# Loads ahead of stores and packing in pieces in a macaron FFN kernel with 4-bit weights

## The chip, the core and the metric

The kernel runs on one core of a Trainium2 chip. A core has a matrix engine (TensorE; PE in the profile, PEld for its weight loads), VectorE (DVE), ScalarE (ACT), GpSimd (POOL) and SyncE (SP), which runs nothing but DMA issues here. Each engine executes its own stream of instructions in order; a semaphore holds an instruction until what it needs is there. The metric is the device time of one execution in microseconds (us), lower is better. The kernel before took 2141.37 us, the median of 2140.46, 2141.37 and 2141.96.

## The reference

The input is `u`, 2 x 1024 tokens of 1024 channels, in f32. Three residual steps follow:

```python
x = u
x = x + 0.5 * ffn(layernorm(x))
x = x + s4(layernorm(x))
x = x + 0.5 * ffn(layernorm(x))

def ffn(x):                      # weights 4-bit, groups of 128 rows
    W = scale[group] * (nibble - (zero[group] + 1))
    return (silu(x @ Wg) * (x @ Wu)) @ Wd     # 1024 -> 2752 -> 1024
```

`s4` is a causal convolution along the 1024 positions with one kernel computed from a state-space model, plus `D[0] * x`. Both FFN calls use the same weights. A word of `qweight` (int32) holds eight nibbles, of eight consecutive rows of one column; `qzeros` packs eight columns a word.

## The kernel before, in words

The 2048 tokens are four blocks of 512. `JOBS` (L1345) lists eight jobs, one for each block and FFN. A job has a gate/up half (`gate_up`, L663) and a down half (`down`, L741). In gate/up, the 43 units of columns are cut into eight waves (`WAVES`, L38): five of six units of 128 columns, two of four, one of five. For each wave the eight groups of 128 input channels are walked (`STEPS`, L39, 64 steps); a step multiplies 512 tokens with the units of the wave for one group, twice (activations are split into a high part `xTh` and a low part `xTl`): 12 matmuls in the first five waves. After each group the partial sums in PSUM are rescaled in place by a ratio of scales (`scaled`, L657 to L661), by ACT for even units and by DVE for most odd ones. The rescaling must end before the next step adds to the same sum. The down half has 44 steps.

The nibbles are unpacked once, in the first job; this text calls it packing. For a wave: `fetch` loads the raw words (L454), `fetch_zeros` the zero points (L461) from a table that `zero_points` (L307) wrote to DRAM; `split` runs six DVE operations (`signed_bytes`, L501); `dequantize` (L541) copies one nibble of all words to bytes on POOL (`q`, L544) and SP stores these to DRAM (`wq`, L545), eight times a wave. A later step loads its 128 rows of bytes (`load_bytes`, L621, four steps ahead), and `make_weights` (three steps ahead) casts them to f32 weights `w_up`, on POOL (L637), or on ACT (L635) for three of eight steps in the first job. All jobs reload the bytes. The loads, stores, words, zero points and scales all stand in SP's one queue of issues. Pools: four `q` buffers, six for bytes, five for weights.

Hooks order this. `at(up, s, f)` runs `f` where step `s` is written; a framework's scheduler orders what the hooks emit by engine, except that `in_order_of_writing(f, engines)` keeps the written order on the engines named. `first_weights` (L579) places packing: a wave's `fetch` at step 8w-15, all six pieces of `split` at 8w-13, and the eight `dequantize` from 8w-12 on, one a step (w = 2 is a step or more off). The scales of later units are loaded (`scale_rows`, L326) in the opening and five steps before steps 16 and 32, and turned and inverted (`scales`, L336 on PE, then DVE) two steps before steps 4, 16 and 32.

`start` (L1519) is the opening, up to step 0, in written order on ACT, DVE, SP and PE. `first_split` splits wave 0's first group of rows in two halves of 16 bits; its `dequantize` copies the eight nibbles, odd ones on POOL (L493) and even ones on ACT (L495); SP stores each twice, 16 rows into the first tile of bytes (L496) and 128 rows to `wq` (L497). `first_moments` takes the layernorm sums of the four token tiles, 1 and 3 on ACT (L1467, L1468), 0 and 2 on DVE (L1473, L1474), then `deviations` the reciprocal roots on DVE. `first_rows` normalizes (ACT for odd tiles, L1488; DVE for even, L1490); `first_turn` transposes a chunk of 128 channels of all four tiles on PE (L1503), ACT makes the high part (L1504), DVE the low part (L1505). Turns 0 and 1 are in the opening; turns 2 to 7, and the rows of the second half of the channels, are hooks of steps 0 to 5 (`rows_by_chunk`, L1507).

Of the kernel before, what the change touches and what calls it, by code (L numbers as in the profile page):

```python
# [24 lines left out]
P = 128  # L25
# [30 lines left out]
def macaron_s4_kernel(  # L56
# [250 lines left out]
    def zero_points(which, z):  # L307

        p, n = z.shape
        zi, tab = (t2(f"{a}_{which}").bitcast(I32)[:p, : 8 * n] for a in ("zi", "ztab"))  # L310
        unpacked_zeros(tab, z, zi)
        dst, seg, queue = (zd_dram, SEGD, nc.sync) if which else (z_dram, SEG, nc.scalar)
        queue.dma_start(dst.rearrange("g (s n) -> (g s) n", s=seg), tab)

    def inverse(inv, s, name):

# [5 lines left out]
    def scale_rows(k0, k1, queue=nc.sync):  # L322
        n = k1 - k0
        row = t4(f"srow_{k0}") if n > 4 else t2(f"srow_{k0}")
        for m, src in enumerate((gate_s, up_s)):
            queue.dma_start(row[m * GK : (m + 1) * GK, : n * P], src[:, k0 * P : k1 * P])  # L326
        return row

    def scales(k0, k1, row):


        n = k1 - k0
        ps = bank(f"ps_s{k0}")
        u0, u1 = 2 * k0, 2 * k1
        for k in range(n):
            nc.tensor.transpose(  # L336
                ps[:, bass.ts(k, 2 * GK)], row[: 2 * GK, bass.ts(k, P)], ident[: 2 * GK, : 2 * GK]
            )
        if k1 == WIDE:
            row = t2("srow_half")  # L340
            for m, src in enumerate((gate_s, up_s)):
                nc.sync.dma_start(row[:GK, m * HALF : (m + 1) * HALF], src[:, WIDE * P :])
            nc.tensor.transpose(ps[:, bass.ts(2 * n, GK)], row[:GK, :P], ident[:GK, :GK])
            u1 = UNITS
        s = s_gu[:, u0:u1]
        flat = lambda a: a.rearrange("p u g -> p (u g)")
        nc.vector.tensor_copy(flat(s), ps[:, : (u1 - u0) * GK])
        inv = t2(f"inv_{k0}")[:, : (u1 - u0) * GK]
        inverse(inv, flat(s), k0)
        own = rat[:, u0:u1]  # L350
        inv = inv.rearrange("p (u g) -> p u g", g=GK)
        nc.vector.tensor_tensor(own[:, :, : GK - 1], s[:, :, : GK - 1], inv[:, :, 1:], ALU.mult)
        nc.vector.tensor_scalar(
            own[:, :, GK - 1 :], s[:, :, GK - 1 :], 1.0 / (EIGHT * LIFT), None, ALU.mult
        )
# [119 lines left out]
    def first_split(zq):  # L475


        n = width_of(0)
        z, zi, even = (t4(f"{a}_w0").bitcast(I32)[:, :n] for a in ("z", "zi", "even"))
        raw = packed.pop(0)[0]  # L480
        unpacked_zeros(z, zq, zi)
        nc.vector.tensor_scalar(even, raw, 3, NIBBLES, ALU.logical_shift_left, ALU.bitwise_and)
        nc.vector.tensor_scalar(raw, raw, 1, NIBBLES, ALU.logical_shift_right, ALU.bitwise_and)
        for part in (even, raw):
            both = part.bitcast(U16)
            nc.vector.tensor_tensor(both, both, z.bitcast(U16), ALU.add)
        nc.vector.tensor_scalar(both, both, 0x8080, None, ALU.bitwise_xor)

        def dequantize(j):
            q = qpool.tile([P, n], I8, tag="q", name=f"q_0_{j}")  # L490
            view = lambda a, dt: a.bitcast(dt).rearrange("p (n k) -> p k n", k=4)[:, j // 2, :]
            if j % 2:
                nc.gpsimd.tensor_copy(q, view(raw, I8))  # L493
            else:
                nc.scalar.activation(q, view(even, U8), AF.Identity, bias=minus_128)  # L495
            nc.sync.dma_start(first_tile[j:P:8], q[: P // 8])  # L496
            nc.sync.dma_start(w_q[0].rearrange("(r j) n -> j r n", j=8)[j], q)  # L497

        return dequantize

    def signed_bytes(key, raw, even, z):  # L501

        nc.vector.tensor_scalar(even, raw, 3, NIBBLES, ALU.logical_shift_left, ALU.bitwise_and)
        yield
        nc.vector.tensor_scalar(raw, raw, 1, NIBBLES, ALU.logical_shift_right, ALU.bitwise_and)
        yield
        for part in (even, raw):
            both = part.bitcast(U16)  # L510
            nc.vector.tensor_tensor(both, both, z.bitcast(U16), ALU.add)  # L511
            yield
            nc.vector.tensor_scalar(both, both, 0x8080, None, ALU.bitwise_xor)
            yield
        view = lambda a: a.bitcast(I8).rearrange("p (n k) -> p k n", k=4)
        packed[key] = view(even), view(raw)

    def split(w):
        raw, z = packed[w]
# [59 lines left out]
    def first_weights(up, dn, at):  # L579


        for w in range(1, len(WAVES)):
            s0 = 8 * w - 12 if w != 2 else 7
            if w > 1:
                both = lambda w=w: (fetch(w), fetch_zeros(w))
                at(up, s0 - 3, lambda both=both: in_order_of_writing(both, ET.SP))
                in_pieces(at, [(up, s0 - 1)], lambda w=w: split(w))
            else:
                both = lambda: [None for _ in split(1)]
                at(up, 0, lambda both=both: in_order_of_writing(both, *STARTING))  # L590
            for j in range(8):
                s = s0 + j if w > 2 else j // 2 + s0 * (w - 1)
                at(up, s, lambda w=w, j=j: dequantize(w, j))
        s0 = len(STEPS) - 12
        when = lambda n: (up, s0 + n) if n < 12 else (dn, (5 * (n - 12)) // 6)
        for n in range(6 * 8):
            k, j = divmod(n, 8)
            a, rt = divmod(k, 3)
            if j == 0:
                at(*when(max(0, n - 7)), lambda a=a, rt=rt: fetch_down(a, rt))  # L600
                steps = [when(max(0, n - d)) for d in (4, 3, 3, 2, 1, 0)]
                in_pieces(at, steps, lambda a=a, rt=rt: split_down(a, rt))
            at(*when(n), lambda a=a, rt=rt, j=j: dequantize_down(a, rt, j))
# [743 lines left out]
    def fast():  # L1347
        for j, (b, k) in enumerate(JOBS):
# [49 lines left out]
                    at(up, 4, store)  # L1398
            if j == 0:
                rows = {3: srow_next}  # L1400
                for s, k0, k1 in ((4, 3, 9), (16, 9, 15), (32, 15, WIDE)):
                    if k0 > 3:
                        load = lambda k0=k0, k1=k1: rows.update({k0: scale_rows(k0, k1)})
                        at(up, s - 5, load)
                    at(up, s - 2, lambda k0=k0, k1=k1: scales(k0, k1, rows.pop(k0)))
                at(up, 40, scales_down)
                zeros = lambda: zero_points(1, zeros_down)
                at(up, 12, lambda: in_order_of_writing(zeros, ET.DVE, ET.SP))
                for c in range(2, NC):
                    more = lambda c=c: rows_by_chunk(c)  # L1410
                    at(up, c - 2, lambda more=more: in_order_of_writing(more, *STARTING))
                first_weights(up, dn, at)
# [43 lines left out]
    STARTING = ET.Activation, ET.DVE, ET.SP  # L1456
    first = {}

    def first_moments():

        stats = small.tile([P, NT, 2, 6], F32, tag="stats", name="stats_0_1")
        mv = small.tile([P, NT, 2], F32, tag="mv", name="mv_0_1")
# [8 lines left out]
        for t in (0, 2):  # L1471
            for i in range(2):
                nc.vector.bn_stats(stats[:, t, i, :], x[0][t][:, bass.ts(i, 512)])  # L1473
            nc.vector.bn_aggr(mv[:, t, :], stats[:, t, :, :].rearrange("p a s -> p (a s)"))  # L1474
        nc.vector.tensor_scalar(mv[:, 1:4:2, 1], squares, 1.0 / HID, None, ALU.mult)
        guess(0, 1, mv)
        return mv, scratch

    def first_rows(t, lo, hi):

        half = lo // 512
        if lo % 512 == 0:
            first[t, half] = t2(f"xn_0_1_{t}_{half}")
        n = first[t, half][:, lo - 512 * half : hi - 512 * half]
        m, r, _ = ln[0, t]
        src = first["x"][t][:, lo:hi]
        if t % 2:
            nc.scalar.activation(n, src, AF.Identity, bias=first["bias"][:, t : t + 1], scale=r)  # L1488
        else:
            nc.vector.tensor_scalar(n, src, m, r, ALU.subtract, ALU.mult)  # L1490

    def first_turn(c):
# [8 lines left out]
        for t in range(NT):  # L1501
            src = first[t, c // 4][:, bass.ts(c % 4, P)]
            nc.tensor.transpose(ps[:, bass.ts(t, P)], src, ident)  # L1503
        nc.scalar.copy(hi, ps)  # L1504
        nc.vector.tensor_tensor(lo, ps, hi.bitcast(F32), ALU.subtract)  # L1505

    def rows_by_chunk(c):  # L1507
        if c < 4:
            for t in (2 * c - 4, 2 * c - 3):
                first_rows(t, 512, HID)  # L1510
        first_turn(c)

    def keep_warm(n, src=None):
# [5 lines left out]
    def start():  # L1519
# [8 lines left out]
        srow = scale_rows(0, 3)  # L1528
        zeros = zero_words(0)
        zeros_down = zero_words(1)  # L1530
        dequantize_first = first_split(zq)
        mv, scratch = first_moments()
        for j in (1, 3, 5, 7, 0, 2, 4, 6):
            dequantize_first(j)
        fetch(1)
        rows_next = scale_rows(3, 9)
# [10 lines left out]
            first_rows(t, P, 512)  # L1547
        scales(0, 3, srow)
        first_turn(1)
        zero_points(0, zeros)  # L1550
        fetch_zeros(1)
        return rows_next, zeros_down

    srow_next, zeros_down = in_order_of_writing(start, *STARTING, ET.PE)
# [88 lines left out]
```

## Time and profile before

| | us |
|---|---|
| median of the runs (three) | 2141.37 |
| the profiled execution | 2140.35 |
| its span | 2138.6 |
| PE busy | 2089.9 (98%) |
| DVE busy | 1700.3 (80%) |
| ACT busy | 1420.2 (66%) |
| POOL busy | 1055.2 (49%) |
| DMA moved, mean rate | 132.14 MB, 62 GB/s |

The profile is of one execution; its span runs from the first recorded instruction to the last. L12 is line 12 of the kernel before. A line of the timeline gives the start, the duration, the engine, the line, the operation, its output and inputs, how many such in a row, and in brackets how long the engine had been idle and what ended that. SPq and ACTq are issues of DMAs: their duration includes what the issue waited for. A line of the waits gives what waited for what, the total in us, how many times, and the longest. A matmul of 128 x 512 takes 0.226 us at full clock; the granted clock is a share of it. Times inside the profile are from the span's start.

### The profile page before, as it was taken

How to read it: one execution, taken by the hardware profiler on the slowest of the kernel's cores; microseconds unless marked ns; L12 is line 12 of the kernel's file. 1: busy time of each engine (PE TensorE's matmuls, PEld its weight loads, DVE VectorE, ACT ScalarE, POOL GpSimd, SP SyncE). 2: the span in 40 equal slices, each digit the busy share in tenths (PEclk: the TensorE clock that was granted, in tenths of full speed). 3: DMA queues.
4: the chain of work that ended last, by engine and by line, in shares of the span. 5: the costliest groups of instructions: out<-in, count | busy, mean ns of one | idle time of the engine just before them, and what ended most of it. 6: DMA issues, size and time to landing. Idle time of an engine off the chain costs nothing.

```text
span 2138.6 us, 30244 instructions
## 1 busy us (share of the span) xinstructions
PE 2089.9 (98%) x9744; PEld 1426.0 (67%) x9744; DVE 1700.3 (80%) x2785; ACT 1420.2 (66%) x2233; POOL 1055.2 (49%) x1424
## 2 busy tenths in 40 slices
PE   6899999999999999999999999999999999999998
PEld 4455675677776578665876568675686766866576
DVE  8888877779888777778777888878788787777776
ACT  6787777746655776676766766547776467767765
POOL 3767848653354543546335543454534545345642
PEclk9999999999999999999999999999999999999999
DMA  4335322112111211212121121112111121121111
GB/s 140 108 87 149 91 81 55 35 55 78 43 38 54 91 51 44 74 32 93 54 81 38 30 72 38 36 52 78 35 37 38 52 97 45 45 81 35 33 35 58
DMA packets 163686, 132.14 MB, mean 62 GB/s; under 512 B 22651, under 2 KB 151172, under 8 KB 163518
## 3 DMA queue, kind: packets, MB, share of 16 engines
q1 hardware_dynamic: 162646, 128.65, 19.8%
q8 instruction: 79, 1.29, 0.3%
q10 hardware_dynamic: 872, 1.47, 0.2%
q14 instruction: 89, 0.73, 0.1%
HBM read 104.45 MB, written 25.50 MB: 61 GB/s over the span
## 4 chain that ended last, share of the span: by engine, by line
PE 89%; DVE 6%; POOL 2%; DMA 1%; issue 1%; ACT 1%; SPq 0%; ACTq 0%; DVEq 0%; POOLq 0%
PE pg L689 54%; PE po L752 27%; PE pc L1078 3%; PE pb L774 1%; DVE pg L661 1%; PE pb L1078 1%; PE pt L228 1%; DVE po L661 1%; PE st L228 1%; DMA wq<-q 0%; DMA z<-z_dram 0%; DVE hf L719 0%; DVE hf_half L733 0%; DVE rawd L511 0%; POOL w_down L637 0%
## 5 line engine op out<-in xcount | busy, mean ns | idle before, releaser
L659 ACT ACTIVATE pg<-pg,rat 128x512 f32<-128x512 f32 x1240 | 786.1, 660 | 426.5 <-PE pg L689 425.5
L661 DVE TENSOR_TENSOR pg<-pg,rat 128x512 f32<-128x512 f32 x1168 | 777.2, 693 | 174.9 <-PE pg L689 170.3
L689 PE MATMUL pg<-xTh,w_up 128*128 128x512 f32 x2752 | 857.8, 439 | 5.2 <-DVE pg L661 4.1
L689 PE MATMUL pg<-xTl,w_up 128*128 128x512 f16 x2752 | 724.0, 383 | 3.2 <-DVE pg L661 1.4
L689 PEld LDWEIGHTS pg<-xTh,w_up 128*128 128x128 f32 x2752 | 520.3, 189 | 180.3 <-DVE pg L661 17.6
L637 POOL CAST w_up<-b 128x768 fp32r<-128x768 int8 (+2 forms) x490 | 375.2, 771 | 535.5 <-PE pg L689 421.6
L752 PE MATMUL po<-hl,w_down 128*128 128x512 f32 x1344 | 539.3, 403 | 8.5 <-DVE po L661 7.0
L659 ACT ACTIVATE po<-po,ratd 128x512 f32<-128x512 f32 x660 | 430.9, 661 | 159.4 <-PE po L752 159.0
L752 PE MATMUL po<-hh,w_down 128*128 128x512 f32 x1344 | 523.0, 392 | 0.0
L661 DVE TENSOR_TENSOR po<-po,ratd 128x512 f32<-128x512 f32 x620 | 427.0, 697 | 97.3 <-PE po L752 93.1
L689 PEld LDWEIGHTS <-w_up 128*128 128x128 bf16 x2752 | 228.3, 99 | 328.6 <-issue 155.9
L637 POOL CAST w_down<-bd 128x512 fp32r<-128x512 int8 x352 | 221.5, 631 | 411.3 <-PE po L752 341.1
L752 PEld LDWEIGHTS po<-hl,w_down 128*128 128x128 f32 x1344 | 252.0, 188 | 85.9 <-DVE po L661 19.8
L752 PEld LDWEIGHTS po<-hh,w_down 128*128 128x128 f32 x1344 | 252.8, 188 | 45.6
L723 POOL TENSOR_TENSOR hl<-hf,hh 128x512 fp32r<-128x512 f32 x168 | 216.8, 1290 | 7.7
L719 DVE SCALAR_TENSOR_TENSOR hf<-pg,rat,g 128x512 f32<-128x512 f32 x168 | 122.9, 747 | 44.9 <-ACT g L716 37.8
L716 ACT ACTIVATE g<-pg,rat 128x512 f32<-128x512 f32 x168 | 110.7, 686 | 49.4 <-PE pg L689 39.6
L721 POOL CAST hh<-hf 128x512 fp32r<-128x512 f32 x168 | 105.9, 630 | 56.0 <-PE pg L689 32.3
L187 DVE BATCH_NORM_STATS2 stats<-x 128x6 f32<-128x512 f32 x88 | 58.5, 676 | 0.5
L1108 DVE TENSOR_TENSOR x<-x,pc 128x512 f32<-128x512 f32 x32 | 21.9, 685 | 36.9 <-PE pc L1078 36.9
L1078 PEld LDWEIGHTS pc<-near,st 128*128 128x128 f32 x256 | 43.6, 191 | 7.9
L776 DVE TENSOR_TENSOR x<-x,pb 128x512 f32<-128x512 f32 x64 | 43.1, 678 | 6.2 <-PE pb L774 6.2
(205 smaller groups left out, 1034.8 us busy)
## 6 DMA issues: line engine op xcount, KB each, us to landing
b<-wq SPq DMA_DIRECT2D x319, 96.0 KB
bd<-wdq SPq DMA_DIRECT2D x336, 64.0 KB
x<-in_L_attn_u_dram SPq DMA_DIRECT2D x30, 512.0 KB
b<-wq SPq DMA_DIRECT2D x128, 64.0 KB
xs<-x SPq DMA_DIRECT2D x16, 512.0 KB
x<-xs SPq DMA_DIRECT2D x16, 512.0 KB
out_dram<-x SPq DMA_DIRECT2D x16, 512.0 KB
b<-wq SPq DMA_DIRECT2D x64, 80.0 KB
```

Of the source, the lines that this page charges most:

```text
L187: nc.vector.bn_stats(stats[:, t, i, :], x[b][t][:, bass.ts(i, 512)])
L637: nc.gpsimd.tensor_copy(t, b)
L659: nc.scalar.activation(dst, src, AF.Copy, scale=sc)
L661: nc.vector.tensor_tensor(dst, src, sc.to_broadcast([P, TB]), ALU.mult)
L689: nc.tensor.matmul(p, weights, (lo, hi)[k][:, g, :], start=(g == 0 and not done), stop=(g == GK - 1 and done), skip_group_check=True,)
L716: nc.scalar.activation(g, pg, AF.Silu, scale=rat[:, 2 * f, GK - 1 :])
L719: nc.vector.scalar_tensor_tensor(hf, pu, last, g, ALU.mult, ALU.mult)
L721: nc.gpsimd.tensor_copy(hi, hf)
L723: nc.gpsimd.tensor_tensor(lo, hf, hi.bitcast(F32), ALU.subtract)
L752: nc.tensor.matmul(ps[c], w[:, bass.ts(c, P)], part, start=(f == 0 and k == 0), stop=(f == NF - 1), skip_group_check=True,)
L776: nc.vector.tensor_tensor(part, part, ps, ALU.add)
L1078: nc.tensor.matmul(dst, lhsT, rhs, start=start, stop=stop, skip_group_check=True)
```

## The change

Packing is rearranged for waves 1 to 7. Wave w + 1's words and zero points are fetched one step after wave w's packing begins (waves 1 and 2 in the opening), in written order on SP, so they stand ahead of that wave's stores. `split` runs in pieces, two at each of three steps from 8w-8 on (35 and 42 for the last two waves), where it was one lump at 8w-13. The eight `dequantize` go in the order 0, 2, 4, 6, 1, 3, 5, 7, three a step from the second of these steps on (one a step in the last two waves). The scales' rows are loaded at steps 6 and 11 (the half unit's row with them, where `scales` loaded it itself) and used at 5, 14 and 30.

In the opening, stores to `wq` go to POOL's queue, those of the first tile stay on SP; ACT copies only nibbles 0 and 2, POOL the other six; the last exclusive-or of the even half (`rest`) and `zero_points(0)` stand between tiles of `first_moments`; the table of zero points is stored by SP, not ACT. All four tiles' rows of the second half go to ACT, two of them in the opening, the others with turns 2 and 3; turns 5, 6 and 7 are copied out by ACT in one piece and split in high and low parts on POOL.

```diff
@@ -309,8 +309,8 @@
         zi, tab = (t2(f"{a}_{which}").bitcast(I32)[:p, : 8 * n] for a in ("zi", "ztab"))
         unpacked_zeros(tab, z, zi)
-        dst, seg, queue = (zd_dram, SEGD, nc.sync) if which else (z_dram, SEG, nc.scalar)
-        queue.dma_start(dst.rearrange("g (s n) -> (g s) n", s=seg), tab)
+        dst, seg = (zd_dram, SEGD) if which else (z_dram, SEG)
+        nc.sync.dma_start(dst.rearrange("g (s n) -> (g s) n", s=seg), tab)
 
@@ -324,12 +324,18 @@
         for m, src in enumerate((gate_s, up_s)):
             queue.dma_start(row[m * GK : (m + 1) * GK, : n * P], src[:, k0 * P : k1 * P])
-        return row
-
-    def scales(k0, k1, row):
+        if k1 < WIDE:
+            return row, None
+        half = t2("srow_half")
+        for m, src in enumerate((gate_s, up_s)):
+            queue.dma_start(half[:GK, m * HALF : (m + 1) * HALF], src[:, WIDE * P :])
+        return row, half
+
+    def scales(k0, k1, rows):
 
         n = k1 - k0
+        row, half = rows
         ps = bank(f"ps_s{k0}")
@@ -337,10 +343,7 @@
             )
         if k1 == WIDE:
-            row = t2("srow_half")
-            for m, src in enumerate((gate_s, up_s)):
-                nc.sync.dma_start(row[:GK, m * HALF : (m + 1) * HALF], src[:, WIDE * P :])
-            nc.tensor.transpose(ps[:, bass.ts(2 * n, GK)], row[:GK, :P], ident[:GK, :GK])
+            nc.tensor.transpose(ps[:, bass.ts(2 * n, GK)], half[:GK, :P], ident[:GK, :GK])
             u1 = UNITS
@@ -486,22 +489,28 @@
             nc.vector.tensor_tensor(both, both, z.bitcast(U16), ALU.add)
         nc.vector.tensor_scalar(both, both, 0x8080, None, ALU.bitwise_xor)
 
+        def rest():
+            upper = even.bitcast(U16).rearrange("p (n k) -> p n k", k=2)[:, :, 1]
+            nc.vector.tensor_scalar(upper, upper, 0x8080, None, ALU.bitwise_xor)
+
         def dequantize(j):
             q = qpool.tile([P, n], I8, tag="q", name=f"q_0_{j}")
             view = lambda a, dt: a.bitcast(dt).rearrange("p (n k) -> p k n", k=4)[:, j // 2, :]
-            if j % 2:
-                nc.gpsimd.tensor_copy(q, view(raw, I8))
+            if j in (0, 2):
+                nc.scalar.activation(q, view(even, U8), AF.Identity, bias=minus_128)
             else:
-                nc.scalar.activation(q, view(even, U8), AF.Identity, bias=minus_128)
+                nc.gpsimd.tensor_copy(q, view(raw if j % 2 else even, I8))
             nc.sync.dma_start(first_tile[j:P:8], q[: P // 8])
-            nc.sync.dma_start(w_q[0].rearrange("(r j) n -> j r n", j=8)[j], q)
-
-        return dequantize
+            nc.gpsimd.dma_start(w_q[0].rearrange("(r j) n -> j r n", j=8)[j], q)
+
+        return rest, dequantize
 
     def signed_bytes(key, raw, even, z):
 
+        view = lambda a: a.bitcast(I8).rearrange("p (n k) -> p k n", k=4)
+        packed[key] = view(even), view(raw)
         nc.vector.tensor_scalar(even, raw, 3, NIBBLES, ALU.logical_shift_left, ALU.bitwise_and)
         yield
         nc.vector.tensor_scalar(raw, raw, 1, NIBBLES, ALU.logical_shift_right, ALU.bitwise_and)
@@ -512,8 +521,6 @@
             nc.vector.tensor_scalar(both, both, 0x8080, None, ALU.bitwise_xor)
             yield
-        view = lambda a: a.bitcast(I8).rearrange("p (n k) -> p k n", k=4)
-        packed[key] = view(even), view(raw)
 
@@ -580,17 +587,15 @@
 
         for w in range(1, len(WAVES)):
-            s0 = 8 * w - 12 if w != 2 else 7
-            if w > 1:
-                both = lambda w=w: (fetch(w), fetch_zeros(w))
-                at(up, s0 - 3, lambda both=both: in_order_of_writing(both, ET.SP))
-                in_pieces(at, [(up, s0 - 1)], lambda w=w: split(w))
-            else:
-                both = lambda: [None for _ in split(1)]
-                at(up, 0, lambda both=both: in_order_of_writing(both, *STARTING))
-            for j in range(8):
-                s = s0 + j if w > 2 else j // 2 + s0 * (w - 1)
-                at(up, s, lambda w=w, j=j: dequantize(w, j))
+            late = w > 5
+            s0 = (8 * w - 8, 42 - 7 * (7 - w))[late]
+            in_pieces(at, [(up, s0 + d) for d in (0, 0, 1, 1, 2, 2)], lambda w=w: split(w))
+            if 1 < w < len(WAVES) - 1:
+                both = lambda w=w: (fetch(w + 1), fetch_zeros(w + 1))
+                at(up, s0 + 1, lambda both=both: in_order_of_writing(both, ET.SP))
+            for i, k in enumerate((0, 2, 4, 6, 1, 3, 5, 7)):
+                s = s0 + 1 + (i if late else i // 3)
+                at(up, s, lambda w=w, k=k: dequantize(w, k))
         s0 = len(STEPS) - 12
         when = lambda n: (up, s0 + n) if n < 12 else (dn, (5 * (n - 12)) // 6)
         for n in range(6 * 8):
@@ -1398,11 +1403,11 @@
                     at(up, 4, store)
             if j == 0:
                 rows = {3: srow_next}
-                for s, k0, k1 in ((4, 3, 9), (16, 9, 15), (32, 15, WIDE)):
+                for first_use, s, k0, k1 in ((5, 0, 3, 9), (14, 6, 9, 15), (30, 11, 15, WIDE)):
                     if k0 > 3:
                         load = lambda k0=k0, k1=k1: rows.update({k0: scale_rows(k0, k1)})
-                        at(up, s - 5, load)
-                    at(up, s - 2, lambda k0=k0, k1=k1: scales(k0, k1, rows.pop(k0)))
+                        at(up, s, lambda load=load: in_order_of_writing(load, ET.SP))
+                    at(up, first_use, lambda k0=k0, k1=k1: scales(k0, k1, rows.pop(k0)))
                 at(up, 40, scales_down)
                 zeros = lambda: zero_points(1, zeros_down)
                 at(up, 12, lambda: in_order_of_writing(zeros, ET.DVE, ET.SP))
@@ -1456,7 +1461,7 @@
     first = {}
 
-    def first_moments():
+    def first_moments(between):
 
@@ -1472,6 +1477,7 @@
                 nc.vector.bn_stats(stats[:, t, i, :], x[0][t][:, bass.ts(i, 512)])
             nc.vector.bn_aggr(mv[:, t, :], stats[:, t, :, :].rearrange("p a s -> p (a s)"))
+            between[t]()
         nc.vector.tensor_scalar(mv[:, 1:4:2, 1], squares, 1.0 / HID, None, ALU.mult)
@@ -1484,7 +1490,7 @@
         m, r, _ = ln[0, t]
         src = first["x"][t][:, lo:hi]
-        if t % 2:
+        if t % 2 or half:
             nc.scalar.activation(n, src, AF.Identity, bias=first["bias"][:, t : t + 1], scale=r)
@@ -1501,13 +1507,18 @@
         for t in range(NT):
             src = first[t, c // 4][:, bass.ts(c % 4, P)]
             nc.tensor.transpose(ps[:, bass.ts(t, P)], src, ident)
-        nc.scalar.copy(hi, ps)
-        nc.vector.tensor_tensor(lo, ps, hi.bitcast(F32), ALU.subtract)
+        if c < 5:
+            nc.scalar.copy(hi, ps)
+            nc.vector.tensor_tensor(lo, ps, hi.bitcast(F32), ALU.subtract)
+        else:
+            both = gpool.tile([P, TB], F32, tag="g", name=f"turn_0_1_{c}")
+            nc.scalar.copy(both, ps)
+            nc.gpsimd.tensor_copy(hi, both)
+            nc.gpsimd.tensor_tensor(lo, both, hi.bitcast(F32), ALU.subtract)
 
     def rows_by_chunk(c):
         if c < 4:
-            for t in (2 * c - 4, 2 * c - 3):
-                first_rows(t, 512, HID)
+            first_rows(2 * c - 4, 512, HID)
         first_turn(c)
 
     def keep_warm(n, src=None):
@@ -1528,9 +1539,11 @@
         zeros = zero_words(0)
         zeros_down = zero_words(1)
-        dequantize_first = first_split(zq)
-        mv, scratch = first_moments()
-        for j in (1, 3, 5, 7, 0, 2, 4, 6):
+        rest, dequantize_first = first_split(zq)
+        for j in (1, 3, 5, 7):
+            dequantize_first(j)
+        mv, scratch = first_moments({0: rest, 2: lambda: zero_points(0, zeros)})
+        for j in (4, 6, 0, 2):
             dequantize_first(j)
@@ -1547,8 +1560,11 @@
         scales(0, 3, srow)
         first_turn(1)
-        zero_points(0, zeros)
+        for t in (1, 3):
+            first_rows(t, 512, HID)
         fetch_zeros(1)
+        fetch(2)
+        fetch_zeros(2)
         return rows_next, zeros_down
```

## The prediction

> **What bounds the kernel now.** I read the engines' shares first (TensorE, PE, 2089.9 us of a span of 2138.6, 98%), then PE's waits over the whole span, busy time by stretch, and the timeline of each engine and of SP's issues in the first 110 us, where the weights are unpacked. PE's waits:
>
> ```profile
> PE warm L1517 <- ACT scratch L1468: 13.6, 1, 13.6
> PE po L752 <- DVE po L661: 7.0, 15, 1.4
> PE pg L689 <- DVE pg L661: 5.5, 7, 1.5
> PE ps_s L336 <- DMA srow<-in_L_ffn_up_scales_dram: 3.3, 1, 3.3
> ```
>
> The change touches the first of the eight jobs only, so its prize is what that job takes above a job with nothing to unpack. Stretches of 20 us (busy time of PE, PEld, DVE, ACT, POOL; granted clock; DMA share; GB/s):
>
> ```profile
> 20.00:40.00 20.00, 15.26 (x76) 9.29 (x77) 19.60 (x41) 13.46 (x23) 10.94 (x13) 0.98 0.35 106
> 40.00:60.00 20.00, 19.61 (x82) 10.32 (x81) 18.34 (x30) 14.78 (x24) 9.95 (x13) 0.93 0.43 124
> 60.00:80.00 20.00, 15.94 (x63) 8.54 (x63) 14.69 (x28) 11.06 (x18) 13.71 (x17) 0.84 0.35 105
> 80.00:100.00 20.00, 19.09 (x84) 10.76 (x84) 18.99 (x32) 15.35 (x25) 14.46 (x17) 0.99 0.39 116
> 120.00:140.00 20.00, 20.00 (x95) 11.95 (x95) 16.64 (x31) 16.42 (x27) 12.96 (x18) 1.00 0.28 79
> ```
>
> The fifth stretch is PE at its pace. The first and third are not: 76 and 63 matmuls instead of 95, the third at a clock of 0.84. I counted the start of each gate/up step (12 matmuls of 0.226 us, 2.71 us) from PE's timeline: step 0 at 21.75, 8 at 53.19, 16 at 83.52, 40 at 150.36, 64 at 203.42. The same stretches of a later job last 21.65, 21.65, 64.96 and about 47.3 us, so the first job loses (beyond the turns it must do) about 7, 8.7, 1.9 and 6 us. Steps 13 and 14 alone took 6.99 and 6.04 us. SP's issues there, then PE:
>
> ```profile
> 54.97 10.92 SPq L545 DMA_DIRECT2D wq<-q  x6
> 65.94 1.23 SPq L454 DMA_DIRECT2D raw<-_L_ffn_gate_qweight_dram  x1
> ...
> 67.75 1.23 SPq L461 DMA_DIRECT2D z<-z_dram  x2
> 69.07 0.88 SPq L545 DMA_DIRECT2D wq<-q  x2
> 70.00 0.38 SPq L326 DMA_DIRECT2D srow<-n_L_ffn_gate_scales_dram  x1
> ```
>
> ```profile
> 74.04 0.79 PE L336 MATMUL ps_s<-ident,srow 16*128 16x16 f32 x6 [3.29 <-DMA srow<-in_L_ffn_up_scales_dram]
> ```
>
> SP's queue is in order: six stores, each waiting for a POOL copy (0.83 us, between POOL's other work), hold SP for 10.92 us; the next wave's words and the scales stand behind them. The row lands after 70 us, PE waits 3.29 us, and its clock is at half from 73.41 to 80.24: half of 6.8 us, 3.4 us, is lost besides. The opening, DVE, ACT and POOL:
>
> ```profile
> 13.47 0.17 DVE L1475 TENSOR_SCALAR mv<-squares 128x2 f32<-128x2 f32 x1 [1.35 <-ACT scratch L1468]
> 23.12 1.51 DVE L290 TENSOR_SCALAR zi<-zq 128x43 int32<-128x43 int32 x8
> 24.66 1.05 DVE L298 TENSOR_SCALAR ztab<-zi 128x688 uint16<-128x688 int32 x1
> ```
>
> ```profile
> 13.34 3.64 ACT L495 ACTIVATE q<-even_w,minus 128x768 int8<-128x768 uint8 x4
> 26.13 0.81 ACT L1488 ACTIVATE xn<-x,bias,r 128x512 f32<-128x512 f32 x1 [1.49 <-DVE ztab L298]
> ```
>
> ```profile
> 20.16 0.83 POOL L637 CAST w_up<-b 128x768 fp32r<-128x768 int8 x1 [8.22 <-DMA b<-q]
> 23.70 3.65 POOL L637 CAST w_up<-b 128x768 fp32r<-128x768 int8 x4 [2.71 <-DMA b<-wq]
> ```
>
> Step 0 waits for rows, a turn and w_up_0 together; SP issues sixteen stores of 0.50 to 0.60 us back to back up to 19.5.
>
> [...] No POOL DMA is in this trace. [...] Here a POOL copy took 1.43 us once instead of 0.83, which fits an engine held up, not more. [...] a reload pays its store's landing: here from the end of wave 1's last copy, 42.34, to the bytes loaded, 46.09, are 3.7 us.
>
> **The change part by part**, for the profiled execution.
>
> (a) *Start to step 0: +1.9.* DVE gets the upper-half xor (0.55, as the 0.56 of its kind) and the zero points (1.51 + 1.05) ahead of the row statistics, 3.1 in all; idle of 0.40 and 1.35 there hides 1.75: +1.4. Eight stores of 0.58 leave SP for POOL's queue, at a cost c of POOL's time each [...]. ACT does two copies instead of four, but these now wait for two of the four q buffers, which come free when the stores behind POOL's third and fourth copies have landed: copies from 8.7 (end of the split), four of 0.83 and four c, 12.0 + 4c, some 1.9 to land (half of the 3.7), 0.92 for the last copy: 14.8 + 4c. Behind them on ACT stand the rows of the first turn, possible at 16.89 + 1.4 = 18.3. At c = 1 they start at 18.8: +0.5 more. Step 0 at 21.75 + 1.9 = 23.65.
>
> (b) *Steps 0 to 8: 31.4 becomes 30.4, −1.0.* The second-half rows (0.81 each) all go to ACT, whose written order becomes three rows, one cast of a turn (0.58), step 0's four scalings (0.61 each) and the fourth row, before the turn that PE has ahead of step 1: with waits about 6.9 us, and 0.4 for the turn: step 1 at 30.9, not 24.88. PE idles 3.7 of this; I add 1.6 for a half clock (a stretch of it from 39.28 to 42.69 cost 1.7 now). Then little is left to wait for: DVE is rid of zero points (2.6), two rows (1.6) and three low parts (2.0), the low parts of three turns going to POOL (0.61 + 1.28 each, as its hh and hl rows). From step 0: 7.3 to step 1, 4.3 for step 1 (2.71 + 1.6), six steps of 2.71 = 16.3, three more turns of 0.45 = 1.35, 0.5 for scales and 0.6 for waits: 30.4.
>
> (c) *Steps 8 to 16: 30.3 becomes 24.0, −6.3.* Loads of words, zero points and scales now stand on SP ahead of the stores of the wave in front, and the scales for step 14 are asked for at step 6. No load waits behind 10.92 us of stores; the 3.29 us wait, its clock loss of 3.4 and the late weights around them go. I keep 2.4 over the 21.65 of a clean stretch: split pieces, scales (0.8 on PE) and one short wait.
>
> (d) *Steps 16 to 40: +1.1.* The packing's six DVE operations (.55 .55 .95 .55 .95 .55, about 4.1 us) come one or two at a time, not as a lump, but between the scalings that free PE's PSUM; DVE is 18.99 of 20 busy from 80 to 100. I count 0.9 to 1.3 a wave against 0.75 to 1.0 now, over three waves: +0.6, and 0.5 for the copies set closer on POOL.
>
> (e) *Steps 40 to 64 and (f) the down half: 0.* Wave 6's weights lose slack (about 10 us to 1.3) but keep some; waves behind are as before. Bound ±2.
>
> (g) *POOL as an issuing engine.* Cost c for each of eight DMAs: at least 0.05 (dispatch alone: an estimate from the 0.05 between the end of one of SP's issues and the next)[...]. Besides (a): six copies of 0.83 from 8.7 and eight c put w_up_0's start at 13.5 + 8c; the reload (3.7) and its cast (0.83) permit step 1 at 18.0 + 8c. At c = 1 that is 26.0, under ACT's 30.9; POOL decides from c = 1.6; the gain is gone at 2.1 to 2.2 by either route.
>
> Sum: +1.9 − 1.0 − 6.3 + 1.1 = −4.3; 2140.35 − 4.3 = 2136.05 for the profiled execution. The median of the runs shown, 2141.37, is 1.0 above that execution: 2137.1.
>
> **Rivals.** That loads and stores don't change places is excluded: in the order as built, SP has each wave's loads ahead of the stores of the wave in front.
>
> *C, ACT's new order doesn't hold step 1.* If PE has step 1's operands by 25 or 26, steps 0 to 8 gain 5 to 6 more: 2131.5. For it: DVE, 19.60 of 20 busy from 20 to 40, bounds that stretch now and is relieved. Against: ACT executes in written order.
>
> *D, a wash.* Copies now wait for splits that end two steps later; the slack of a wave's first weights is about 3 us (bytes landed 18.0 us after the wave in front starts, needed at 21). If each of four waves loses 1.2 us to that, 2137.1 + 4.8 = 2142.
>
> *A, slower: POOL's DMA issue.* Place: the opening; price: c. [...] it is slower by 0.2% from c = 2.7. For: eight DMAs behind one engine that makes the first weights, beside a DVE that is 19.60 of 20 busy. Against: nothing in this trace prices them.
>
> *B, slower: POOL's copies.* Should they run at the 1.43 us seen once, eight add 4.8 us to a wave, past its 3 us of slack: 2 us and a half clock, 2.5 to 3.5, for each of four waves: 2147 to 2151.
>
> **Chances and range.** Mine 0.42 (own range 2133 to 2140), C 0.13, D 0.15, A 0.17, B 0.13. Faster or slower by over 0.2% (4.3 us, about what a measurement of this kernel can tell from no change) means under 2137.1 or over 2145.6. Mine lies on the line, so half of it and C are faster, 0.36; its other half and most of D the same, 0.31; A, B and D's worse end slower, 0.33. From C's 2131 to A's 2149, which leaves out B's upper part and the tails of A and C, under 0.2.
>
> **What would show it.** (a) step 0 near 23.6; (b) step 1 near 31, with ACT's three rows, four scalings and a row ahead of it, and a half clock after; (c) no store holding SP for 10 us ahead of words or scales, steps 13 and 14 at about 2.7 us, clock from 60 to 80 near 1.00; (d) DVE waits at waves' first steps of about 1 us[...]. Wrong would make me: a POOL DMA over 1.6 us, a wave's first weights late, or ACT's order not being what PE waits for.

## The result, and the profile after

The changed kernel took 2150.8 us (median of five, 2149.97 to 2152.14) against 2140.94 (five runs): ratio 1.0047, interval 1.0033 to 1.0062. It is slower by about 10 us; 2137.1 was predicted, with a range up to 2149. The profiled execution took 2150.77, its span 2148.9. All of the loss arises in the first job: at the start of every later job the changed kernel stands 9.9 to 10.2 us behind.

The starts of the steps of the first job, counted from PE's timeline as in the prediction, give the lengths of its parts:

| part | before | predicted | after |
|---|---|---|---|
| start to step 0 | 21.75 | 23.65 | 24.03 |
| steps 0 to 8 | 31.4 | 30.4 | 29.6 |
| steps 8 to 16 | 30.3 | 24.0 | 26.2 |
| steps 16 to 40 | 66.8 | 67.9 | 77.4 |
| steps 40 to 64 | 53.1 | 53.1 | 56.1 |
| down half | 96.0 | 96.0 | 96.0 |

Up to step 16 the change had gained 3.7 us. Steps 16 to 40 lost 10.6, where 1.1 was expected, and steps 40 to 64 another 3.0. The stretches of 20 us after (busy PE, PEld, DVE, ACT, POOL; clock; DMA share; GB/s):

```profile
20.00:40.00 20.00, 18.41 (x84) 12.08 (x83) 16.00 (x29) 15.79 (x26) 10.96 (x12) 1.00 0.47 133
40.00:60.00 20.00, 18.94 (x85) 10.46 (x84) 15.67 (x25) 15.48 (x25) 16.18 (x18) 1.00 0.35 104
60.00:80.00 20.00, 17.71 (x78) 9.85 (x78) 18.51 (x36) 12.69 (x22) 12.68 (x14) 1.00 0.34 104
80.00:100.00 20.00, 18.94 (x82) 10.50 (x79) 18.11 (x26) 13.71 (x23) 16.84 (x17) 1.00 0.18 60
100.00:120.00 20.00, 16.11 (x61) 8.53 (x59) 13.79 (x20) 12.95 (x21) 13.54 (x14) 0.91 0.25 74
120.00:140.00 20.00, 19.01 (x87) 10.72 (x86) 16.25 (x28) 15.43 (x25) 12.30 (x16) 1.00 0.33 98
```

The third stretch has 78 matmuls instead of 63 and a clock of 1.00 instead of 0.84: that gain came. The stretch from 100 to 120 was full before:

```profile
100.00:120.00 20.00, 20.00 (x91) 11.79 (x88) 16.26 (x28) 16.38 (x27) 15.42 (x19) 1.00 0.36 107
```

Now it has 61 matmuls and a clock of 0.91, and the one from 120 to 140 has 87 instead of 95. PE's waits over the whole span, after:

```profile
PE warm L1528 <- ACT scratch L1473: 13.4, 1, 13.4
PE po L757 <- DVE po L666: 6.4, 13, 1.3
PE pg L694 <- DVE pg L666: 6.3, 14, 0.9
PE pg L694 <- ACT pg L664: 6.1, 7, 3.0
...
PE pg L694 <- POOL w_up L642: 1.2, 1, 1.2
```

The wait of 3.29 us for scales is gone. In its place is a wait for one of ACT's scalings, 3.0 us at its longest (1.1 in all before), and waits for DVE's scalings are 14 instead of 7. The long one, on PE and then on ACT:

```profile
103.90 1.16 PE L694 MATMUL pg<-xTl,w_up 128*128 128x512 f16 x3 [2.98 <-ACT pg L664]
```

```profile
98.04 0.66 ACT L664 ACTIVATE pg<-pg,rat 128x512 f32<-128x512 f32 x1 [0.37 <-PE pg L694]
102.46 0.83 ACT L640 CAST w_up<-b 128x768 fp32r<-128x768 int8 x1 [3.76 <-DMA b<-wq]
103.19 1.81 ACT L664 ACTIVATE pg<-pg,rat 128x512 f32<-128x512 f32 x3
```

PE stands at the end of step 22: step 23 adds to sums that ACT must scale first. These scalings could run, but ahead of them in ACT's order stands the cast of group 1 of the next wave (step 25, made three steps ahead), which waits 3.76 us for its bytes. After these 2.98 us of idle time the clock is lower too: half speed from 104.41 to 107.82 (0.50 granted). Why the bytes are late, on SP:

```profile
64.31 7.51 SPq L552 DMA_DIRECT2D wq<-q  x8
...
77.36 0.42 SPq L457 DMA_DIRECT2D raw<-_L_ffn_gate_qweight_dram  x1
...
90.75 6.81 SPq L552 DMA_DIRECT2D wq<-q  x8
99.06 4.63 SPq L626 DMA_DIRECT2D b<-wq  x8
```

The order of loads and stores is as intended: words are asked for at 77.36, before that wave's stores. But the stores end 17.7 us after step 16 (which starts at 79.85), and the copies 17.4 us after it; the bytes that the cast of group 1 waits for come 22.6 us after it. VectorE and GpSimd in the 12 us from step 16 on, where GpSimd also makes the `hh` and `hl` rows, the high and the low part of the products `hf` that the wave just ended has left for the down half:

```profile
81.51 0.55 DVE L514 TENSOR_SCALAR even<-raw 128x768 int32<-128x768 int32 x1
82.10 1.51 DVE L516 TENSOR_SCALAR raw<-raw 128x768 int32<-128x768 int32 x1
83.53 1.28 DVE L666 TENSOR_TENSOR pg<-pg,rat 128x512 f32<-128x512 f32 x2
84.72 1.52 DVE L520 TENSOR_TENSOR even<-even,z 128x1536 uint16<-128x1536 uint16 x1
...
88.43 1.60 DVE L520 TENSOR_TENSOR raw<-raw,z 128x1536 uint16<-128x1536 uint16 x1
```

```profile
81.61 1.58 POOL L728 TENSOR_TENSOR hl<-hf,hh 128x512 fp32r<-128x512 f32 x1
83.14 0.94 POOL L726 CAST hh<-hf 128x512 fp32r<-128x512 f32 x1
84.15 1.28 POOL L728 TENSOR_TENSOR hl<-hf,hh 128x512 fp32r<-128x512 f32 x1
85.38 1.34 POOL L726 CAST hh<-hf 128x512 fp32r<-128x512 f32 x1
86.80 1.66 POOL L728 TENSOR_TENSOR hl<-hf,hh 128x512 fp32r<-128x512 f32 x1
...
101.76 0.83 POOL L642 CAST w_up<-b 128x768 fp32r<-128x768 int8 x1 [4.54 <-DMA b<-wq]
```

Pieces of the split that took 0.55 and 0.95 take 1.51, 1.52 and 1.60; hh rows of 0.61 take 0.94 and 1.34, hl rows of 1.28 up to 1.66. The piece at 82.10 ends 0.42 us after the row that it met, those at 84.72 and 88.43 0.81 us after a row and after a cast of weights. It goes both ways: the hh row at 83.14 came second and ended 0.47 us after the piece at 82.10. VectorE's scalings, whose sums lie in PSUM, took 0.68 to 0.69 us there and 0.69 in the mean of the span. By what the two engines hold each other up no run here shows. The split's six operations sum to 6.3 us, where those of the second and third wave took 4.2 and 4.1 before. Before, the split stood in the later half of a wave, where no hh or hl row runs, and these rows kept 0.61 and 1.28:

```profile
70.61 0.55 DVE L507 TENSOR_SCALAR raw<-raw 128x768 int32<-128x768 int32 x1
74.71 0.95 DVE L511 TENSOR_TENSOR raw<-raw,z 128x1536 uint16<-128x1536 uint16 x1
```

```profile
59.58 0.61 POOL L721 CAST hh<-hf 128x512 fp32r<-128x512 f32 x1
60.93 1.28 POOL L723 TENSOR_TENSOR hl<-hf,hh 128x512 fp32r<-128x512 f32 x1
```

### The profile page after: what moved, and what is told of

Its sections match the earlier page's. It is cut to its first block, busy times and chain, and to the rows that moved or that the text cites. A ratio compares the mean times of both kernels' runs of the same rounds, so it can differ in the third digit from the quotient of the medians.

```text
span 2148.9 us, 30248 instructions
## 1 busy us (share of the span) xinstructions
PE 2095.6 (98%) x9744; PEld 1426.8 (66%) x9744; DVE 1705.8 (79%) x2781; ACT 1419.9 (66%) x2233; POOL 1075.2 (50%) x1440
## 4 chain that ended last, share of the span: by engine, by line
PE 87%; DVE 7%; POOL 1%; ACT 1%; issue 1%; DMA 1%; SPq 0%; DVEq 0%; ACTq 0%; POOLq 0%
PE pg L694 52%; PE po L757 27%; PE pc L1083 3%; DVE pg L666 2%; PE pb L779 1%; PE pb L1083 1%; DVE po L666 1%; PE pt L228 1%; POOL q L551 1%; PE st L228 1%; DMA b<-wq 1%; DVE hf L724 0%; ACT g L721 0%; ACT pg L664 0%; DVE rawd L520 0%
```

## The experiments

The theories were: (1) split and rows holding each other up; (2) the opening; (3) the split in pieces between scalings, without GpSimd; and, when the runs asked for it, (4) packing too near its use however fast it runs, and (5) ScalarE's cast passing late bytes on to PE.

**Each half alone.** First the kernel before with `first_weights`, the scales' steps and the early `packed` of the change, and the second wave's words loaded at step 1:

```diff
-            s0 = 8 * w - 12 if w != 2 else 7
+            s0 = (8 * w - 8, 42 - 7 * (7 - w))[late]
...
+            if w < len(WAVES) - 1:
+                both = lambda w=w: (fetch(w + 1), fetch_zeros(w + 1))
+                at(up, s0 + 1, lambda both=both: in_order_of_writing(both, ET.SP))
```

> The packing of waves 1 to 7 and the loads of words, zero points and scales as in the changed kernel, the opening as before. In the changed kernel steps 8 to 64 took 159.7 us, before 150.2. Theory 1 (split on VectorE and the hh and hl rows on GpSimd, both in the first 9 us of a wave, hold each other up, so the copies end 3 us later and the next wave's first weights are late) and theory 3 (split in pieces delays the scalings, without GpSimd having a part): about 2150, 9 above the kernel before. Theory 2 (the loss comes from the opening, GpSimd's store issues among it): about 2141.

2149.86, ratio 1.0040 (1.0026 to 1.0054). Steps 16 to 40 took 77.9 us. Then the changed kernel with `first_weights` and the scales' steps of the kernel before:

```diff
-            s0 = (8 * w - 8, 42 - 7 * (7 - w))[late]
+            s0 = 8 * w - 12 if w != 2 else 7
...
-        fetch(2)
-        fetch_zeros(2)
```

> The opening as in the changed kernel, packing and scales as before. At step 8 the changed kernel stood 0.4 us behind. Theories 1 and 3: 2139 to 2144. Theory 2: about 2150. Ten loads ahead of the second group's bytes become six, so step 1 may start near 29 instead of 30.5.

2142.97, ratio 1.0010 (1.0001 to 1.0019). The loss lies in the waves; theory 2 explains 1 to 2.5 us at most.

**The same packing four steps earlier.**

```diff
-            s0 = (8 * w - 8, 42 - 7 * (7 - w))[late]
+            s0 = (8 * w - 8 - 4 * (w > 1), 42 - 7 * (7 - w))[late]
```

> The changed kernel with the packing of waves 2 to 5 four steps (10.8 us) earlier, behind the hh and hl rows of a wave instead of beside them; same work. Theory 1: VectorE's six operations of these waves back at about 4.1 us in sum (6.3 in the changed kernel), hh at 0.61 and hl at 1.28, last copy 3 us or more ahead of need, steps 16 to 40 back to 66 to 69 us (77.4), the time 2138 to 2143. Theory 3: the pieces still stand between scalings, 2147 to 2151. Lack of GpSimd time as such: also 2147 to 2151.

2136.43, ratio 0.9979 (0.9969 to 0.9988): faster than both kernels, and than both expectations. Steps 16 to 40 took 67.1 us, the third wave's six split operations sum to 4.1 us (the second's to 5.4, the fourth's to 4.5), and hh and hl rows in the waves concerned keep 0.61 and 1.28. The stretch that had 61 matmuls is full again:

```profile
100.00:120.00 20.00, 20.00 (x94) 12.02 (x93) 16.07 (x28) 16.54 (x27) 15.29 (x20) 1.00 0.32 96
```

The split is still in pieces between scalings, so theory 3 falls. But packing is now both undisturbed and earlier, and this run doesn't separate the two.

**The order of loads alone.** In the kernel before:

```diff
-                at(up, s0 - 3, lambda both=both: in_order_of_writing(both, ET.SP))
+                at(up, max(8 * w - 20, 0), lambda both=both: in_order_of_writing(both, ET.SP))
...
-                for s, k0, k1 in ((4, 3, 9), (16, 9, 15), (32, 15, WIDE)):
+                for first_use, s, k0, k1 in ((5, 0, 3, 9), (14, 6, 9, 15), (30, 11, 15, WIDE)):
```

> The kernel before with nothing changed but where loads stand: a wave's words and zero points ahead of the stores of the wave in front, and the scales' rows at steps 6 and 11, used at 5, 14 and 30. The part of the prediction that valued this, steps 8 to 16, came to -6.3; measured with the rest of the change -4.1. If the order of loads is worth that by itself: 2135 to 2137. If the wait only moves to the weights behind it: 2139 to 2142.

2138.69, ratio 0.9992 (0.9986 to 0.9999). Steps 8 to 16 fell from 30.3 to 28.0, and steps 16 to 24 rose from 22.9 to 25.1: most of the gain was handed on to the next wave's weights. At step 16 a cast of them on ScalarE waited 2.96 us for its bytes, and PE 2.20 us for the scaling behind that cast, which is theory 5's path in another kernel. Between the two expectations, nearer the second.

**Split early, copies late**, in the kernel that packs four steps earlier, meant to part theories 1 and 4:

```diff
-                s = s0 + 1 + (i if late else i // 3)
+                s = s0 + 1 + (i if late else i // 3) + 4 * (1 < w < 6)
```

> As the kernel with packing four steps earlier, but only the split is earlier; GpSimd's copies of waves 2 to 5 stand at the steps where the changed kernel has them. Theory 1 (split and hh or hl rows hold each other up; without it hh and hl end by 6.5 us of a wave and copies by 14 to 15, not 17.4, in time for loads needed at 21): 2137 to 2141, hh and hl at 0.61 and 1.28. Theory 4 (the copies stand too near their use, however fast they run): PE's wait of 3 us at step 22 stays, 2147 to 2151.

2137.16, ratio 0.9984 (0.9976 to 0.9993). Inconclusive: where copies stand on GpSimd is left to the scheduler, and those of the third to fifth wave ran within 1.5 us of where the kernel with all packing earlier has them, counted from the start of a wave.

**The hh and hl rows moved instead.** Everything as changed; only these rows of four waves (put into `rows`) stand behind the copies:

```diff
+        if j == 0 and f < 12:
+            later.append(rows)
+        else:
+            rows()
...
+                for w in range(1, 5):
+                    for i in range(3):
+                        low = lambda: in_order_of_writing(later.pop(0), ET.Pool)
+                        at(up, 8 * w + 4 + i, low)
```

> The changed kernel with split, copies and loads where it has them; only the hh and hl rows of the first four waves stand behind the copies on GpSimd (steps 4 to 6 of the next wave instead of 0 to 3). Theory 1 (split and these rows meeting is the cause): the six VectorE operations of waves 2 to 5 at about 4.1 us, last copy 14 to 15 us after the wave in front starts instead of 16.4 to 17.9, no wait of 3 us at step 22, the time 2139 to 2143. Theory 4 (packing stands too near its use however fast it runs) or theory 3 (pieces between scalings): 2148 to 2152.

2144.48, ratio 1.0016 (1.0008 to 1.0023): half way. VectorE from the same step 16 on:

```profile
81.45 0.56 DVE L516 TENSOR_SCALAR raw<-raw 128x768 int32<-128x768 int32 x1
81.93 1.29 DVE L666 TENSOR_TENSOR pg<-pg,rat 128x512 f32<-128x512 f32 x2
83.12 0.95 DVE L520 TENSOR_TENSOR even<-even,z 128x1536 uint16<-128x1536 uint16 x1
```

The operations shown are back at 0.56 and 0.95 (one of the six still took 1.27; the sum is 4.5), the last copy ends at 14.5 us instead of 17.4, as theory 1 said, and steps 16 to 40 fall from 77.4 to 72.0. (At step 43 one piece of the last wave's split now takes 5.60 us beside moved rows and other work of GpSimd; that is this edit's own cost: the step takes 9.79 us, 3.21 in the changed kernel.) PE's waits in steps 16 to 40, in the changed kernel and then here:

```profile
PE pg L694 <- ACT pg L664: 3.6, 2, 3.0
PE pg L694 <- DVE pg L666: 2.5, 7, 0.7
```

```profile
PE pg L694 <- ACT pg L664: 3.1, 2, 2.7
PE pg L694 <- DVE pg L666: 0.3, 1, 0.3
```

The waits for VectorE are gone. But the wait for ScalarE that theory 1 was to remove is there still, with the cast before it:

```profile
99.89 0.83 ACT L640 CAST w_up<-b 128x768 fp32r<-128x768 int8 x1 [3.50 <-DMA b<-wq]
```

So theory 1 is about half of it. Copies 3 us earlier bring the bytes of group 1 only 2.1 us earlier, 20.5 us after step 16 instead of 22.6, and PE, no longer held up by VectorE, also starts step 22 earlier, at 16.3 instead of 18.2.

**ScalarE's casts moved.** In the changed kernel, ScalarE casts groups 4, 5 and 6 of a wave instead of 1, 2 and 5:

```diff
-        if j == 0 and stage == "up" and s > 2 and s % GK in (1, 2, 5):
+        if j == 0 and stage == "up" and s > 2 and s % GK in (4, 5, 6):
```

> The changed kernel; ScalarE's three casts of weights in a wave are those of its groups 4, 5 and 6 instead of 1, 2 and 5, so that no cast which waits for a new wave's bytes stands ahead of step 22's scalings in ScalarE's queue. Theory 5 (late bytes reach PE through that cast): the wait of 2.98 us at step 22 and its half clock go, steps 16 to 40 at 71 to 74 us instead of 77.4, VectorE's operations still stretched, the time 2144 to 2147. If the bytes themselves hold PE: the wait moves to step 24, 2149 to 2151.

2140.06, ratio 0.9993 (0.9984 to 1.0002): as fast as the kernel before, a gain larger than expected. PE's waits from 80 to 153 us, steps 16 to 40, are only

```profile
PE pg L694 <- DVE pg L666: 1.9, 5, 0.5
```

Steps 16 to 40 took 70.9 us, 40 to 64 52.8. The split's operations are as stretched as ever (6.1 us), which leaves 4 of the 10.6 us; the last copy ends at 15.3, 2 us earlier than in the changed kernel, since GpSimd makes fewer weights at a wave's start. That this by itself isn't the reason is seen in two places. With the rows moved the last copy ended earlier still, and the wait stayed. And here GpSimd's cast of group 1 begins at 102.53, when its bytes land, 21.0 us after step 16 begins; the scalings of step 22, which in the changed kernel stood behind that cast, had begun 2 us before on ScalarE:

```profile
100.47 1.24 ACT L664 ACTIVATE pg<-pg,rat 128x512 f32<-128x512 f32 x2 [0.43 <-PE pg L694]
```

The bytes are late here too, and no longer reach PE through ScalarE. Theory 4 falls with this, since packing stands where the change put it. The control, the same line in the kernel before:

> Control: the kernel before with nothing changed but ScalarE's casts, groups 4, 5 and 6. Its copies have bytes ready 10 us ahead in waves 3 and 4, so no cast waits there: 2139 to 2142. If the choice of casts is worth something by itself, outside this range.

2138.42, ratio 0.9988 (0.998 to 0.9997): the casts alone are worth some 2.4 us there, just outside what was expected; in the changed kernel 10.7. Less these 2.4, some 8 us are what the casts cost the changed packing. Both edits together:

> The same, and the hh and hl rows of the first three waves behind the copies. If meeting and cast are the two causes of the loss from step 16 to 40: that stretch at 66 to 69 us, the time 2138 to 2142. If something else is missing: 2144 or more.

2141.19, ratio 1.0005 (0.9995 to 1.0014), steps 16 to 40 72.8: not additive. Steps 16 to 24 took 21.9 us (28.4 in the changed kernel, 22.9 before), so there the two leave nothing of the loss; the new loss is in steps 24 to 32, at 27.6. The moved rows hold the three `hf` buffers, and VectorE's next products wait for them, which delays the scalings behind:

```profile
101.90 0.75 DVE L726 SCALAR_TENSOR_TENSOR hf<-pg,rat,g 128x512 f32<-128x512 f32 x1 [1.33 <-POOL hl L731]
104.45 0.75 DVE L726 SCALAR_TENSOR_TENSOR hf<-pg,rat,g 128x512 f32<-128x512 f32 x1 [1.81 <-POOL hl L731]
```

**The opening.** The changed kernel's GpSimd (with eight stores), then VectorE:

```profile
10.40 1.27 POOL L504 DMA_DIRECT2D wq<-q  x2
14.52 1.84 POOL L502 COPY q<-even_w 128x768 int8<-128x768 int8 x2
16.32 2.13 POOL L504 DMA_DIRECT2D wq<-q  x4
29.62 4.51 POOL L642 CAST w_up<-b 128x768 fp32r<-128x768 int8 x4 [9.04 <-DMA b<-wq]
```

```profile
14.85 0.78 DVE L1481 TENSOR_SCALAR mv<-squares 128x2 f32<-128x2 f32 x1
15.66 0.73 DVE L195 TENSOR_SCALAR ve<-mv 128x4 f32<-128x4 f32 x1
```

A GpSimd issue takes 0.54 us in the median of the eight, 0.79 at most (0.53 to 0.66 in the mean of a line above). Two operations of 0.17 took 0.78 and 0.73 beside the copies at 14.52, and each ended 0.03 us after a copy. Five runs with packing four steps earlier vary the opening. Their steps are read from one profile each, and six profiles with the changed kernel's opening put step 1 between 6.5 and 7.6 us after step 0. The second wave's words at step 1, not ahead of the bytes of group 1:

```diff
-        fetch(2)
-        fetch_zeros(2)
...
-            if 1 < w < len(WAVES) - 1:
+            if w < len(WAVES) - 1:
```

> The kernel that packs four steps earlier, with the second wave's words and zero points loaded at step 1 instead of in the opening, so six issues instead of ten stand ahead of the bytes of group 1. The prediction's reason for step 1 at 30.5 was ScalarE's order: then step 1 stays at 30 to 30.5 and the time at 2136 to 2137. If the bytes' landing (29.6 in the changed kernel) holds it as much: step 1 at 28.5 to 29.5, the time 2135.

2133.0, ratio 0.9960 (0.9946 to 0.9975). GpSimd's second weights come at 26.20 instead of 29.56, and from step 0 to step 1 is 5.3 us instead of 7.0. In this profile step 0 came 1.1 us later, so step 1 started at 29.8, not in the range written, though the time fell. Then rows 0 and 2 of the second half on VectorE, and all four ahead of step 0:

```diff
-        if t % 2 or half:
+        if t % 2:
```

> The same, and besides two of the four second-half rows go back to VectorE, all four ahead of step 0. If ScalarE's rows were what step 1 waited for: step 1 at 27 to 28, the time 2133 to 2135. If not: no difference from the kernel with the second words later.

2131.39, ratio 0.9954 (0.9937 to 0.9970), step 1 4.6 us after step 0, at 28.8: later than the range written, and the time below it. The 0.7 us of that way is within the scatter, and which of the two moves counts isn't separated. The stores back on SP in that kernel:

```diff
-            nc.gpsimd.dma_start(w_q[0].rearrange("(r j) n -> j r n", j=8)[j], q)
+            nc.sync.dma_start(w_q[0].rearrange("(r j) n -> j r n", j=8)[j], q)
```

> The kernel with rows on VectorE (2131.4) and the eight stores of the first group back on SP's queue. A GpSimd issue measured 0.53 to 0.66 us in the changed kernel, an SP issue 0.58. If the second queue is worth what it takes off SP: SP's sixteen issues reach further, bytes of group 1 come 2 to 3 us later, step 1 at 30 or later, 2133 to 2135. If freeing GpSimd and VectorE's small operations (two of them took 0.75 instead of 0.17 beside it) is worth more: 2129 to 2131.

2132.74, ratio 0.9960 (0.9946 to 0.9974), its interval overlapping: step 0 comes at 21.9 instead of 24.2, step 1 at 28.4 instead of 28.8. The second queue decides nothing that these runs can tell. The old opening with the waves four steps earlier:

> The opening of the kernel before with the waves of the kernel that packs four steps earlier. With the waves of the changed kernel the two openings differed by 0.9 us in the median and by 1.6 at step 16, the old one ahead. If this holds: 2134 to 2136. If the old opening, where VectorE has more to do in steps 0 to 5, pays for the second wave's split at steps 4 to 6: 2137 to 2140.

2131.73, ratio 0.9953 (0.9937 to 0.9970), below both ranges; and with the low parts of turns 5 to 7 on GpSimd,

> The old opening with waves four steps earlier (2131.7), and the low parts of turns 5 to 7 on GpSimd as in the changed kernel. If VectorE is what steps 2 to 6 wait for there: 1.5 to 3 us faster, 2129 to 2130. If GpSimd, which also makes the first weights and copies, is: no gain or 1 to 2 slower.

2134.27, ratio 0.9966 (0.9953 to 0.9978): no gain. Several versions beat both kernels; the fastest two, 2131.4 and 2131.7, differ in the opening and share the waves.

## Why the prediction was wrong

*Start, (a): right in sum, +1.9 against +2.3, partly for another reason.* ScalarE's copies, counted as 0.5, held nothing up (the second ended at 17.3, the row that followed waited for VectorE). The rest came from VectorE: two small operations took 1.2 us more in sum than 0.17 each.

*Steps 0 to 8, (b): −1.9 against −1.0.* Step 1 came at 30.5, as predicted (30.9). That the sum is near is partly luck: step 0 to step 1 took 6.5 us, not 7.3, and step 1 took 2.7, not 4.3, since PE's clock wasn't halved there (1.00 from 24 to 34), while steps 2 to 8 took 20.4, not 18.8. And ScalarE's order was only one of two holders: group 1's bytes, behind ten issues, were cast at 29.6 to 30.4. Moving words and then rows took 1.8 and 0.7 us off the way from step 0 to step 1, the second within the scatter.

*Steps 8 to 16, (c): −4.1 against −6.3.* The scales' wait and its clock loss went as stated. Step 13 took 4.53 us, not 2.71, and steps 9 to 11, where the second wave's split meets rows, 10.1, against 8.2 with the rows moved. With packing four steps earlier this part took 22.3 us. Steps 0 to 8 took 33.6 in that profile, but PE's clock was at half from 29.69 to 33.10 there; with the second words later the two parts took 29.9 and 22.9.

*Steps 16 to 40, (d), failed: +10.6 against +1.1.* The prediction costed the split's operations at the durations that they had in the later half of a wave and placed them, unchanged, beside the hh and hl rows. They sum to 6.3 us instead of 4.1, GpSimd's rows and copies are stretched with them, and taking the rows away gave 5.4 us of that part back. The trace before held a sign of it: the fourth wave's split met casts of weights there, two of its pieces took 1.15 and 1.57 us and the six 5.3; and GpSimd copies of 1.43 to 1.49 us came in three waves, not once. The second error is the slack of 3 us under rivals B and D, bytes landed at 18.0 and needed at 21. In the changed kernel the bytes of group 1 came at 22.6. Need was counted at PE's first use of the weights. The casts on ScalarE come three steps ahead, in front of scalings that PE needs at once: with the rows moved, step 22 starts at 16.3, so PE wants its scaled sum at 19.0 (16.3 + 2.71), and a scaling of 0.66 and the cast of 0.83 come before that: by this estimate bytes were needed at 17.5, and there was no slack even at 18.0. Moving these casts gave 6.5 us back (0.9 in the kernel before). The two overlap (5.4 and 6.5 against 10.6).

*Steps 40 to 64, (e), failed: +3.0 against 0.* The runs point to the same two causes in shorter waves: 52.8 us with the casts moved, 50.8 with packing earlier. Two casts on ScalarE wait 1.8 us each for bytes there in the changed kernel, none with the casts moved. How much each of the two counts wasn't separated, and the kernel before gained 1.5 us there from the casts alone.

*Rivals.* A is out: an issue from GpSimd took 0.54 us of its time in the median and 0.79 at most, below the c = 1 that the sum used, and landed in 1.9 us in the median. The c = 1, and the price behind A's 2149, the upper end of the range, were the author's assumptions; the trace before showed neither. C is out, step 1 did wait. B named the time, 2147 to 2151, and lateness of a wave's first bytes, but put it on copies of 1.43 us each; the copies summed to 7.6 to 7.9 us a wave against 7.2 before, and it was the rows and the split ahead of them, and the cast behind, that made up the rest. D's loss of 1.2 us a wave was of the right kind and too small. One sum of the chances is off: half of 0.42 and 0.13 make 0.34, not 0.36.

## What to carry to other kernels

A duration read in one place did not hold here beside other neighbours (a piece of 0.55 us took 1.51, an hh row of 0.61 took 1.34): before moving a VectorE operation, look at what GpSimd does in the new place, and cost both with the stretch that the trace shows where they already meet. The slack of a wave's first bytes ended at the first instruction that waited for them in ScalarE's order, not at the last consumer: the cast waited 3.76 us, and PE 2.98 for the scalings behind it. Look at what stands behind that instruction. Here the cheapest mend was to let ScalarE cast groups whose bytes had long arrived, or to pack four steps earlier; the two together were not run.

## What the runs showed of the hardware

VectorE operations of two and four elements a partition were held up beside GpSimd copies as larger ones were: 0.78 and 0.73 us instead of 0.17. One held operation sat out several of GpSimd's: the piece of 5.60 us, with the rows moved (the next of its size took 0.48), started at 156.31 and ended at 161.91, 0.34 us after the last of seven GpSimd operations that followed each other without a gap.

In three places PE's clock was at half for 3.4 us from within 1 us of the end of a wait: in the kernel before from 39.28 to 42.69, where a wait of 2.21 us ended at 38.36; in the changed kernel from 104.41 to 107.82, where one of 2.98 us ended at 103.90; with the rows moved from 102.19 to 105.60, where one of 2.74 us ended at 101.33, and six matmuls that took 1.73 us elsewhere took 2.88. These are single profiles, in which other idle time near by may have counted.
